# A selective scan on one core: the first stage in an order written by hand, half of a convolution moved into the first scan unit, two row blocks per bank in heads, evictions placed by chunk

## The chip, the cores and the metric

The kernel runs on one core of a Trainium2 chip. Five engines work at once: PE (TensorE) multiplies and transposes, DVE (VectorE), ACT (ScalarE) and POOL (GpSimd) work element by element, and SP (SyncE) issues most of the DMAs. All wait for each other through semaphores. The metric is the time of one execution in microseconds (us); less is better.

## The reference

Layer 0 is a convolutional state space block, layer 1 attention and a mixture of experts. Only layer 0 is touched. Cut to what matters (float32, 4 images of 32 x 32 pixels, 256 channels; Dn = 512, N = 64 states, R = 16):

```python
x = _layernorm(src, ln1_g, ln1_b)
x = x @ w_in + b_in                                   # (4, 32, 32, 512)
x = conv3x3_depthwise(x, conv_w) + conv_b
x = jax.nn.gelu(x).reshape(B, L, Dn)                  # L = 1024
proj = x @ w_x
dt_raw, Bm, Cm = jnp.split(proj, [R, R + N], axis=-1)
dt = jax.nn.softplus(dt_raw @ w_dt + dt_bias)
A = -jnp.exp(A_log)
# over the 1024 pixels:
h = jnp.exp(dt[:, :, None] * A) * h + (dt * x)[:, :, None] * Bm[:, None, :]
y = jnp.einsum('bdn,bn->bd', h, Cm)
# then
y = _layernorm(y + x * D_skip, ln2_g, ln2_b)
out = src + y @ w_out + b_out
```

## The kernel before

**Units and slots.** Work on layer 0 is cut into 8 units: each image has two halves of 512 pixels (`TPB` = 4 row blocks of 128 pixels; `NT` = 8 per image). A unit has 64 states times 4 blocks of 128 channels (`DK` = 4), so 256 slots, and each slot is one scan over 512 pixels on DVE (`scan`, L967). The channels lie on the partitions.

What one slot needs: ACT makes the decay `da` = exp(dt x A) (`decay`, L941) and the scaled input `bx` (`scale`, L921, one per row block of 128 pixels with the pixels on the partitions and 512 channels across); PE turns four 128 x 128 pieces of `bx` into a PSUM bank `ps` (`turn`, L953; there are three such banks); DVE scans; after four slots POOL multiplies the state by C (L978) in one instruction of 128 x 2048; PE adds the result up over the states in four banks `y0` to `y3` (`add_up`, L992). For the first row block of a state, a string `KINDS` says who scales: `A` ACT, `P` POOL (`scale_apart`, L932), `D` PE itself by a diagonal matrix read from DRAM (`turn`, L948; the diagonals are written as entries into `diag_b`, which has to be zero elsewhere).

**The slot loop** (L1126 to L1181) issues the instructions in the order in which they run on each engine; nothing is reordered (`manual_schedule`). Slot k issues `scale` for k + 8, `decay` for k + 4, the scan of k, `add_up` for k − 11 and `turn` for k + 3.

**Work beside the scans.** Between these the loop places pieces of other work for later and earlier units. `beside` makes lists of pieces, each with an engine, an assumed cost and a window of slots (`EVEN`, `ODD`, and `START` for unit 0). `MOST` limits what one slot takes on an engine. Pieces that need a bank all use one, `bg`: "take" claims it, "free" gives it back at the eviction. The pieces are:

- `head(b, g)`: for a half image, rows scaled by the layernorm's 1/sigma (ACT), turned by PE (L339), evicted to `xT` (L344), multiplied by `w_in` (L364), evicted with the bias to `pad` (L375), an image with a border of zeros.
- `conv(v)`: the convolution of unit v as products with diagonal matrices: 9 taps for each of the 4 channel blocks, 36 in all (L417). Three diagonals at a time lie in a tile `dgc` (three buffers). For unit 0 DVE makes them (L401) and they are kept in DRAM as `diags` (L404); later units load them (L406). A tap is 512 wide when the stage runs alone and two of 256 beside scans (`parts`). The result goes to `xg` (L431, L435), then gelu on ACT.
- `dt_bc(w)`: the projections (L470), their turns (L486, L498), dt's products (L541), softplus in several steps (`sum_up` on POOL), the turn of dt x (L595) and its eviction to `dtxT` (L600, L564).
- `after(u)`: layernorm and the product with `w_out` for the unit just ended.

`on_scalar(what)` tells whether an eviction is on ACT or DVE, by its name and the unit's parity (`APART`).

**The first stage** (before the first scan) runs through the same pieces, one list after the other, under a scheduler that works out the order. `late_weights` prepares `w_out`; `head_stats` computes mean and variance of all rows, for the images 1 to 3 from 24 loads of 128 KB.

```python
        head_stats(0, 1)
        run(head(0, 0))
        run(head(0, 1, 0, 1))
        run(conv(0))
        run(head(0, 1, 1, TPB))
        dt_0 = dt_bc(0, None)
        run(*dt_0[:2])
        conv_1 = conv(1)
        ...
        head_stats(1, NB)
        late_weights()
```

`conv(0)` needs half an image and one more row block. `conv(1)` is whole in the first stage, although unit 1 alone needs it. During unit 0 the loop issues `zero_part` on SP, once in each of the first 16 states: a write of 512 KB of zeros into `diag_b`.

Of the kernel before, what the change touches and what calls it, by code (L numbers as in the profile page):

```python
# [33 lines left out]
def conv_ssm_attn_moe_kernel(ctx: ExitStack, tc: tile.TileContext, a: dict, out: bass.AP):  # L34
# [110 lines left out]
    with ExitStack() as l0:  # L145
# [11 lines left out]

        x_0 = pre.tile([P, NT, C], F32, name="x_0", tag="e")
        for g in range(NHALF):
            nc.sync.dma_start(out=x_0[:, blk(g, TPB), :], in_=rows(xf, 0)[:, blk(g, TPB), :])  # L160
        g1 = load_column("L0_conv_ln1_g", CK, w0)
        b1 = load_column("L0_conv_ln1_b", CK, w0)
        w_in = load_rows("L0_conv_w_in", CK, DN, w0)
        b_in = load_column("L0_conv_b_in", DK, w0)
        cw = w0.tile([P, DK, 9], F32, name="cw")
        with nc.allow_non_contiguous_dma(reason="small, once"):
            for m in range(DK):
                nc.scalar.dma_start(
                    out=cw[:, m, :],
                    in_=a["L0_conv_conv_w"][:, :, 0, m * P : (m + 1) * P].rearrange(  # L170
                        "i j p -> p (i j)"
                    ),
                )
        cb = load_column("L0_conv_conv_b", DK, w0)
# [9 lines left out]
        A = load_rows("L0_conv_A_log", DK, NS, w0)  # L184
        nc.scalar.activation(A, A, AF.Exp)
        nc.vector.tensor_scalar(A, A, -1.0, None, ALU.mult)
        dsk = load_column("L0_conv_D_skip", DK, w0)
        g2 = load_column("L0_conv_ln2_g", DK, w0)
        b2 = load_column("L0_conv_ln2_b", DK, w0)
        nc.sync.dma_start(out=w_o, in_=a["L0_conv_w_out"].rearrange("(k p) n -> p k n", p=P))  # L190
        nc.scalar.dma_start(out=b_o, in_=a["L0_conv_b_out"].partition_broadcast(P))
# [16 lines left out]

        pbi = bank()
        for m in range(DK):  # L210
            for ck in range(CK):
                nc.tensor.matmul(
                    pbi[:, m : m + 1], w_in[:, ck, blk(m, P)], b1[:, ck : ck + 1],
                    start=(ck == 0), stop=(ck == CK - 1),
                )
        nc.vector.tensor_tensor(b_in, pbi[:, :DK], b_in, ALU.add)
        centre(w_in, CK, DN, g1)


# [30 lines left out]

        part_of = NS // 8

        def zero_part(i):
            k, n = 1 - i // 8, (i % 8) * part_of
            nc.sync.dma_start(
                out=diag_b[k][n : n + part_of].rearrange("n a b -> a n b"),
                in_=over_middle(zero, part_of),
            )
# [43 lines left out]
        def head_stats(b0, b1):  # L302
            n = (b1 - b0) * NT
            mv = pre.tile([P, n, 2], F32, name="mv_h", tag=f"mv_h{n}")
            for b in range(b0, b1):
                for i in range(NT):
                    t = x_0[:, i, :]
                    if b:
                        t = pre.tile([P, C], F32, name="xs", tag="xr", bufs=2)
                        nc.sync.dma_start(out=t, in_=rows(xf, b)[:, i, :])  # L310
                    variance(mv[:, (b - b0) * NT + i, :], t, C)
            rs = rs_h[:, b0:b1, :].rearrange("p b g -> p (b g)")
            logs(rs, mv[:, :, 1])
            roots(rs, mv[:, :, 1], n)

# [8 lines left out]
        def head(b, g, lo=0, hi=TPB):  # L324
# [11 lines left out]
            def turned(i, ck):  # L336
                if ck == 0:
                    take()
                nc.tensor.transpose(made["bg"][:, blk(ck, P)], made["xn", i][:, blk(ck, P)], ident)  # L339

            def put(i):
                if i == lo:
                    made["xT"] = pre.tile([P, CK, BANK], F32, name="xT")
                (nc.scalar.copy if on_scalar("xT") else nc.vector.tensor_copy)(  # L344
                    made["xT"][:, :, blk(i, P)],
                    made["bg"][:, : CK * P].rearrange("p (k t) -> p k t", k=CK),
                )

            for i in range(lo, hi):
                todo.append(piece(6 if i == lo else 1, "ACT", 0.4, lambda i=i: scaled_rows(i)))  # L350
                todo.append(piece(
                    2, "PE", 0.22, lambda i=i: (turned(i, 0), turned(i, 1)), "take"
                ))
                todo.append(piece(
                    2, "ACT" if on_scalar("xT") else "DVE", 0.42, lambda i=i: put(i), "free"
                ))

            cut = [(lo, hi)] if alone else [(lo, (lo + hi) // 2), ((lo + hi) // 2, hi)]

            def mult(m, ck, i):  # L360
                if ck == 0 and i == 0:
                    take()
                p, q = cut[i]
                nc.tensor.matmul(  # L364
                    made["bg"][:, (p - lo) * P : (q - lo) * P], w_in[:, ck, blk(m, P)],
# [3 lines left out]
            def put_pad(m):  # L369
                pad = pads[m][:, 1 + g * ROWS + lo * RPT : 1 + g * ROWS + hi * RPT, 1 : 1 + WW]  # L370
                bg = made["bg"][:, : (hi - lo) * P].rearrange("p (h w) -> p h w", w=WW)
                if on_scalar("pad"):
# [3 lines left out]

            for m in range(DK):
                for i in range(len(cut)):
                    for ck in range(CK):
                        todo.append(piece(  # L380
                            1, "PE", 1.03 / len(cut), lambda m=m, ck=ck, i=i: mult(m, ck, i),
                            "" if ck or i else "take",
                        ))
                todo.append(piece(
                    3, "ACT" if on_scalar("pad") else "DVE", 0.7, lambda m=m: put_pad(m), "free"
                ))
            return todo

        def conv(v):
# [19 lines left out]
            parts = 1 if alone else 2  # L409
# [14 lines left out]
            def put(m):  # L424
# [3 lines left out]
                if on_scalar("xg"):  # L428
# [13 lines left out]
            for m in range(DK):  # L442
                for k in range(9):
# [10 lines left out]
                    3, "ACT" if on_scalar("xg") else "DVE", 0.69, lambda m=m: put(m), "free"  # L454
# [4 lines left out]
        def dt_bc(w, needs):  # L459
# [15 lines left out]
            def put_pair(j):  # L475
                if j == 0:
                    made["proj", w] = acts.tile([P, TPB, RX], F32, name="proj")
                (nc.scalar.copy if on_scalar("pair") else nc.vector.tensor_copy)(
# [23 lines left out]
            def put_bc():  # L502
# [4 lines left out]
                made["bct", w] = t  # L507
                made["cd", w] = cd
                done.add(("bct", w))

            for j in range(TPB):
# [5 lines left out]
                if j % 2:  # L517
                    todo.append(piece(
                        3, "ACT" if on_scalar("pair") else "DVE", 0.5,
# [59 lines left out]
            def sum_up(m, k):  # L579
                e, dt = made["e"][:, m, :], made["dt", w][:, m, :]  # L580
                eng = nc.vector if alone else nc.gpsimd
                if k == 0:

                    eng.tensor_tensor(e, e, made["s"][:, m % 2, :], ALU.add)
# [14 lines left out]
            def put_dtx(m):  # L599
                (nc.scalar.copy if on_scalar("dtx") else nc.vector.tensor_copy)(  # L600
# [17 lines left out]
            todo = []  # L618
            for m in range(0, DK, 2):
                todo.append(piece(1, "ACT", 1.5, lambda m=m: one_more(m)))  # L620
# [9 lines left out]
            for m in range(DK):  # L630
                todo.append(piece(4 if m == 0 else 1, "PE", 0.44, lambda m=m: turn_dtx(m), "take"))
                todo.append(piece(
                    2, "ACT" if on_scalar("dtx") else "DVE", 0.69,
# [4 lines left out]
        def entries(w):  # L638

            def part(i):  # L640
                with nc.allow_non_contiguous_dma(reason="diagonals"):
                    nc.sync.dma_start(
                        out=diag_b[w % 2].rearrange("n a b -> n (a b)")[
                            blk(i, part_of), :: P + 1
                        ],
                        in_=made["bct", w][blk(i, part_of), :P],
# [20 lines left out]
        def after(u, need):  # L667
# [20 lines left out]
            def put(j):  # L688
                t = pre.tile([P, DK, P], F32, name="yT")
                (nc.scalar.copy if on_scalar("yT") else nc.vector.tensor_copy)(  # L690
# [1544 lines left out]
```

## Time and profile before

| | |
|---|---|
| Time, median of 3 runs | 3336.74 us (3336.47 to 3341.86) |
| Time of the profiled execution | 3336.55 us |
| Its span, first to last instruction | 3334.8 us |
| Mean granted TensorE clock | .989 |
| First stage, to the first scan | 129.06 us |
| Units 0 to 7, from first scan to first scan | 316.67, 321.06, 316.29, 321.46, 316.48, 320.09, 319.62, 308.52 us |
| Layer 1, after the last scan | 665.6 us |

Busy time by stage, from the view of windows (us from the span's start, length, then busy us and number of instructions on each engine, granted clock, share of the DMA engines' time and GB/s):

```profile
core 0: us, PE busy (x) PEld busy (x) DVE busy (x) ACT busy (x) POOL busy (x), PEclk, DMA share, GB/s
0.00:35.40 35.40, 20.90 (x63) 11.75 (x64) 19.54 (x70) 5.14 (x10) 6.16 (x15) 0.90 0.56 131
35.40:66.30 30.90, 30.90 (x75) 13.54 (x74) 16.48 (x63) 0.54 (x2) 1.27 (x5) 1.00 0.43 130
66.30:89.10 22.80, 17.16 (x72) 10.35 (x70) 9.86 (x18) 4.12 (x5) 0.00 (x0) 0.93 0.07 20
89.10:117.40 28.30, 28.24 (x73) 13.12 (x74) 16.04 (x27) 10.47 (x9) 0.00 (x0) 0.94 0.39 115
117.40:129.10 11.70, 11.16 (x40) 6.62 (x38) 4.00 (x12) 11.63 (x16) 2.06 (x3) 1.00 0.00 0
```

These stretches are the head, conv 0, the rest of the head with the projections and dt, conv 1 with softplus beside it, and the last steps to the first scan. "PE" is TensorE's matmuls, "PEld" its loading of weights, which overlaps them. A float32 matmul of 512 columns leaves two records.

### The profile page before, as it was taken

The numbers are of one execution on the slowest core, as the hardware profiler recorded it, in microseconds if no ns is written. First come the engines' busy times: TensorE is split into PE (matmuls) and PEld (weight loads), VectorE is DVE, ScalarE is ACT, GpSimd is POOL, SyncE is SP. The second block draws the span as 40 slices with busy tenths as digits, with TensorE's granted clock in tenths as the row PEclk, the third lists the DMA queues.
The fourth block names the chain that finished last, engine by engine and source line by source line (L and its number), as shares of the span: only waits on it lengthen the run. The fifth ranks groups of instructions, "written<-read, shape, count | busy, mean of one in ns | idle before, by whom it ended". The sixth has DMA issues, their size and how long they took to land.

```text
span 3334.8 us, 62828 instructions
## 1 busy us (share of the span) xinstructions
PE 3158.7 (95%) x23407; PEld 2747.8 (82%) x23407; DVE 2895.5 (87%) x3437; ACT 2716.5 (81%) x4621; POOL 2718.2 (82%) x1216
## 2 busy tenths in 40 slices
PE   7999999999999999999999999989999999899998
PEld 4688988988898888888989888778777766589998
DVE  4799999999999999999999999999999967752222
ACT  1799999999999999999999999999999855322221
POOL 0499998999999989999999999999999943344443
PEclk9999999999999999999999999989999999899999
DMA  4352222222333222233332222322212121477785
GB/s 106 106 120 66 69 67 68 70 70 69 63 77 70 72 69 75 62 67 72 75 72 69 69 66 61 76 52 70 61 59 69 54 66 51 154 198 231 218 252 147
DMA packets 424396, 300.77 MB, mean 90 GB/s; under 512 B 225633, under 2 KB 329953, under 8 KB 424082
## 3 DMA queue, kind: packets, MB, share of 16 engines
q1 hardware_dynamic: 397762, 274.25, 30.1%
q0 software_dynamic: 14016, 18.05, 2.9%
q10 hardware_dynamic: 12304, 4.37, 0.5%
q8 instruction: 187, 3.06, 0.4%
q14 instruction: 127, 1.04, 0.1%
HBM read 262.34 MB, written 34.87 MB: 89 GB/s over the span
## 4 chain that ended last, share of the span: by engine, by line
ACT 42%; PE 37%; DVE 11%; issue 4%; POOL 3%; DMA 2%; SPq 0%; DVEq 0%; POOLq 0%; ACTq 0%
ACT da L941 21%; ACT bx L921 18%; DVE h L967 7%; PE ps L953 7%; PE p L1976 7%; PE y L992 7%; PE pf L1991 3%; PE bg L417 3%; POOL h L978 2%; PE ps L417 2%; PE pqk L1354 1%; PE ps L948 1%; PE ps L364 1%; DMA dgb<-diag_b 1%; PE bg L470 0%
## 5 line engine op out<-in xcount | busy, mean ns | idle before, releaser
L978 POOL TENSOR_TENSOR h<-h,cb_n 128x2048 f32<-128x2048 f32 x511 | 2143.2, 4203 | 117.0 <-DVE h L967 74.7
L941 ACT ACTIVATE da<-dt,l_conv_a_log_sb 128x512 f32<-128x512 f32 x2048 | 1435.5, 712 | 18.6 <-DVE h L967 17.6
L921 ACT ACTIVATE bx<-dtxT,proj 128x512 f32<-128x512 f32 x1748 | 1244.3, 712 | 29.1 <-DVE dtxT L600 16.4
L992 PE MATMUL y<-ident,h 128*128 128x128 f32 x8192 | 1236.1, 274 | 5.8 <-POOL h L978 2.7
L967 DVE TENSOR_TENSOR_SCAN h<-da,last,ps 128x512 f32<-128x512 f32 x1024 | 1217.7, 1258 | 7.2 <-PE ps L953 2.1
L967 DVE TENSOR_TENSOR_SCAN h<-da,ps 128x512 f32<-128x512 f32 x1024 | 1168.9, 1201 | 19.7 <-PE ps L953 7.6
L953 PE MATMUL ps<-ident,bx 128*128 128x128 f32 x6992 | 1117.9, 275 | 41.6 <-DVE h L967 31.1
L992 PEld LDWEIGHTS y<-ident,h 128*128 128x128 f32 x8192 | 978.9, 141 | 96.0 <-issue 20.0
L953 PEld LDWEIGHTS ps<-ident,bx 128*128 128x128 f32 x6992 | 820.0, 142 | 100.0 <-DVE h L967 82.0
L1983 DVE TENSOR_TENSOR hT<-s,p 128x256 f32<-128x256 f32 x146 | 61.5, 421 | 276.7 <-ACT s L1982 248.7
L2001 POOL DMA_INDIRECT out_dram<-yb,src x73 | 116.0, 1589 | 204.0 <-DVE yb L1998 71.9
L953 PE MATMUL ps<-ident,bxp 128*128 128x128 f32 x800 | 236.4, 295 | 44.9 <-DVE h L967 32.4
L1982 ACT ACTIVATE s<-p 128x256 f32<-128x256 f32 x146 | 56.1, 384 | 260.8 <-PE p L1976 239.7
L417 PE MATMUL bg<-pad,dgc 128*128 128x256 f32 x864 | 258.1, 380 | 0.6 <-DMA dgc<-diags 0.6
L953 PEld LDWEIGHTS ps<-ident,bxp 128*128 128x128 f32 x800 | 112.1, 140 | 125.9 <-DVE h L967 74.1
L932 POOL TENSOR_SCALAR bxp<-dtxT,proj 128x512 f32<-128x512 f32 x200 | 141.2, 706 | 59.3 <-DVE dtxT L600 59.3
L948 PE MATMUL ps<-dgb,dtxT 128*128 128x128 f32 x800 | 171.4, 296 | 19.1 <-DMA dgb<-diag_b 9.2
L1976 PE MATMUL p<-xT,w 128*128 128x128 f32 x1408 | 173.5, 277 | 2.2 <-ACT xT L1956 2.2
L1976 PEld LDWEIGHTS p<-xT,w 128*128 128x128 f32 x1408 | 169.0, 193 | 5.1 <-ACT xT L1956 3.0
L948 PEld LDWEIGHTS ps<-dgb,dtxT 128*128 128x128 f32 x800 | 120.5, 190 | 46.7 <-DVE h L967 34.3
L417 PEld LDWEIGHTS bg<-pad,dgc 128*128 128x128 f32 x864 | 130.5, 191 | 0.8 <-DMA dgc<-diags 0.8
L1976 PE MATMUL p<-xT,m 128*128 128x128 f32 x928 | 113.2, 275 | 0.0
(343 smaller groups left out, 2675.4 us busy)
## 6 DMA issues: line engine op xcount, KB each, us to landing
cb_n<-cd SPq DMA_DIRECT2D x512, 256.0 KB
m<-in_L_ffn_w_dram SPq DMA_DIRECT2D x87, 512.0 KB
w<-in_L_ffn_w_dram SPq DMA_DIRECT2D x60, 512.0 KB
dgc<-diags SPq DMA_DIRECT2D x84, 192.0 KB
diag_b<-zero SPq DMA_DIRECT2D x16, 512.0 KB
dgb<-diag_b SPq DMA_DIRECT2D x100, 64.0 KB
last<-h SPq DMA_DIRECT2D x256, 2.0 KB
xd<-xe SPq DMA_DIRECT2D x8, 512.0 KB
```

Of the source, the lines that this page charges most:

```text
L417: nc.tensor.matmul(made["bg"].rearrange("p (h w) -> p h w", w=WW)[:, blk(c, deep), :], made["dgc", m * 3 + i][:, j, :], pads[m][:, at : at ...
L921: nc.scalar.activation(t, made["dtxT", u][:, j, :], AF.Copy, scale=made["proj", u][:, j, R + n : R + n + 1])
L932: nc.gpsimd.tensor_scalar(t, made["dtxT", u][:, 0, :], made["proj", u][:, 0, R + n : R + n + 1], 1.0, ALU.mult, ALU.mult,)
L941: nc.scalar.activation(t, made["dt", u][:, m, :], AF.Exp, scale=A[:, m, n : n + 1])
L948: nc.tensor.matmul(t[:, blk(j, P)], made["dtxT", steps[s][0]][:, j, blk(m, P)], made["dgb", s], start=True, stop=True,)
L953: nc.tensor.transpose(t[:, blk(j, P)], made["bx", s, j][:, blk(m, P)], ident)
L967: nc.vector.tensor_tensor_scan(h[:, m, 1:], made.pop(("da", s, m)), made.pop(("dbx", s, m)), 0.0 if seg == 0 else last[b][:, n, m : m + 1] ...
L978: nc.gpsimd.tensor_tensor(h[:, :, :BANK], h[:, :, 1:], over_middle(made["c", s], DK), ALU.mult)
L992: nc.tensor.matmul(made["y", u][j][:, blk(m, P)], made["h", s][:, m, blk(j, P)], ident, is_transpose=True, start=n == 0 and m == 0, stop=n ...
L1976: nc.tensor.matmul(p12[:, j, s, :], w_of(w, key)[:, ck, blk(h + j, P)], on_b["xT", key][:, ck, :], start=(ck == 0), stop=(ck == CK - 1),)
L1991: nc.tensor.matmul(on_b["pf", key], on_b["hT", key][:, hk, :], w_of("w3", key)[:, hk, :], start=(hk == 0), stop=(hk == HK - 1),)
L2001: s = nc.gpsimd.indirect_dma_start(of[:, :], bass.IndirectOffsetOnAxis(src[:, c : c + 1], 0), yb, None, bounds_check=NB * L - 1, oob_is_er ...
```

## The change

**The first stage** is written out by hand, under `manual_schedule`. The first half of the image is loaded, then `w_in`, then the second half; `cw` is loaded on SP's queue instead of ACT's; ACT's table is loaded first; small loads come later. `w_in` is scaled into `w_s` and centred from there. The rows are scaled in place, and two blocks share a bank when turned (`turn_x0`). Each channel block is evicted by ACT and DVE in turn (`put_rows`). In conv 0, `triple` issues three taps; beside them stand the statistics of the other images' rows, now loaded in 12 DMAs of 256 KB into the scan's ring (`other_rows`), the 16 zero writes (two after each of the first six triples, then one), the turns of the late rows and `late_weights`. Gelu reads PSUM directly, block by block, and the projections are accumulated block by block (`project_0`). Softplus is split over ACT, DVE and POOL. Of conv 1, two channel blocks (18 taps) fill PE's gaps (`filler`).

**Unit 0.** The other 18 taps of conv 1 are a new list `rest` in slots 11 to 20, with taps 512 wide. The zero writes are gone from the slot loop. Two of the first `bx` are made by DVE.

**Heads** turn two row blocks into one bank and evict both at once: two evictions of 128 x 512 instead of four of 128 x 256.

**Placing.** `on_scalar` takes the chunk as well (`pad1`, `xT3`), and `APART` has a third row for unit 0. `KINDS` has a row for unit 0 (37 states on POOL, 29 before), and two other rows are edited. Most windows of `EVEN`, `ODD` and `START` move; POOL's limit in `MOST` is 1.1. In unit 1's softplus ACT's step is done one channel block at a time.

```diff
+        nc.scalar.preload_act_table_set("natural_log_exp_and_others")
         x_0 = pre.tile([P, NT, C], F32, name="x_0", tag="e")
...
-            for i in range(lo, hi):
-                todo.append(piece(6 if i == lo else 1, "ACT", 0.4, lambda i=i: scaled_rows(i)))
+            for i in range(lo, hi, 2):
+                n = min(2, hi - i)
...
+                todo.append(piece(2, "PE", 0.22 * n, lambda i=i, n=n: turned(i, n), "take"))
                 todo.append(piece(
-                    2, "PE", 0.22, lambda i=i: (turned(i, 0), turned(i, 1)), "take"
+                    2, "ACT" if on_scalar("xT", i) else "DVE", 0.1 + 0.3 * n,
+                    lambda i=i, n=n: put(i, n), "free",
                 ))
...
-            parts = 1 if alone else 2
+            parts = 1 if alone or v in (1,) else 2
...
-            return not alone and what in APART[made["u"] % 2]
+            return not alone and f"{what}{part}" in APART[made["u"] % 2 if made["u"] else 2]
...
-            return 2 if u + 1 == len(units) else u % 2
+            return 3 if u == 0 else 2 if u + 1 == len(units) else u % 2
...
                 if u == 0:
+                    rest = conv(1)
+                    cut = [i for i, p in enumerate(rest) if p[4] == "free"][PRE_CONV - 1] + 1
                     lists.append([
-                        (head(b, 0), at["head"]), (head(b, 1), at["head1"]), (conv(v), at["conv"]),
+                        (rest[cut if PRE_CONV else 0 :], at["rest"]), (head(b, 0), at["head"]),
+                        (head(b, 1), at["head1"]), (conv(v), at["conv"]),
                     ])
...
-            'ADADAAPAAAPAAAPAAAPADAPADAAAAPPPDAPADAPADAPAADADDPPPDPPPDPPPDAPA',
+            'ADADAAPAAAPAAAPAAAPADAPADPPPDPPPDPPPPAADAPAADADDPPPAPPPDPPPDAPA',
+            'DPPPPPPAPPPPPPPPPPPPPPPPAPPPPPPAAAAPAAPAAAPAAAAAAAAAAPAPAPAPAPAP',
...
         START = {
-            'skip': (13, 54),
-            'head': (11, 36),
-            'head1': (44, 75),
-            'conv': (43, 228),
+            'skip': (54, 126),
+            'rest': (11, 20),
+            'head': (16, 88),
+            'head1': (90, 102),
+            'conv': (120, 248),
...
+        def triple(m, i, ps):
+            q = 3 * m + i
+            if q + 2 < 3 * DK:
+                taps_0[q + 2]()
+            for j in range(3):
+                nc.tensor.matmul(
+                    ps.rearrange("p (h w) -> p h w", w=WW), made["dgc", q][:, j, :],
+                    pads[m][:, i : i + ROWS, j : j + WW],
+                    start=(i + j == 0), stop=(i + j == 4),
+                )
+
+        for b in range(1, NB):
+            other_rows(b)
+        zeros = iter(range(16))
+        late = None
+        for m in range(DK):
+            ps = spare(m)
+            for i in range(3):
+                triple(m, i, ps)
+                at = NT + 2 * (3 * m + i)
+                for t in range(at, min(at + 2, NB * NT)):
+                    variance(mv_h[:, t, :], row_of(t), C)
+                for _ in range(2 if m < 2 else 1):
+                    for t in (next(zeros, None),):
+                        if t is not None:
+                            zero_part(t)
...
+            nc.scalar.activation(xg[:, m, :], ps, AF.Gelu_apprx_tanh, bias=cb[:, m : m + 1])
+            if m == 1:
+                pp = spare(0), ps_w.tile([P, BANK], F32, name="bg", tag="bg", bufs=1)
+                project_0(0)
+            elif m == 2:
+                project_0(1)
+                for k in range(DK):
+                    t = bank()
+                    project_in(k, t[:, : (TPB - 1) * P], xT_2, 1, TPB)
+                    put_rows(k, TPB + 1, NT, t[:, : (TPB - 1) * P], k % 2)
+            elif m == 3:
+                project_0(2)
...
+        filler(11)
+        cd = made["cd", 0] = dram0.tile([NS, BANK], F32, name="cd")
+        nc.sync.dma_start(out=cd, in_=last_of[NS:, :])
+        for s in range(4):
+            fetch(s)
+        turn_dtx0(1)
+        filler(2)
...
-                if k % DK == 2 and k // DK < 16:
-                    zero_part(k // DK)
```

## The prediction

> **What bounds the kernel now.** I read first the page's engine totals and costliest groups. The groups give three rows that the sum uses again and again.
>
> ```profile
> PE 3158.7 (95%) x23407; PEld 2747.8 (82%) x23407; DVE 2895.5 (87%) x3437; ACT 2716.5 (81%) x4621; POOL 2718.2 (82%) x1216
> ...
> L941 ACT ACTIVATE da<-dt,l_conv_a_log_sb 128x512 f32<-128x512 f32 x2048 | 1435.5, 712 | 18.6 <-DVE h L967 17.6
> L921 ACT ACTIVATE bx<-dtxT,proj 128x512 f32<-128x512 f32 x1748 | 1244.3, 712 | 29.1 <-DVE dtxT L600 16.4
> ...
> L967 DVE TENSOR_TENSOR_SCAN h<-da,ps 128x512 f32<-128x512 f32 x1024 | 1168.9, 1201 | 19.7 <-PE ps L953 7.6
> ```
>
> PE's 95% doesn't say what a stage is worth, so I cut the span at the first scan of each unit (129.06, 445.72, 766.78 and so on) with the view of windows. Units 0 to 2:
>
> ```profile
> core 0: us, PE busy (x) PEld busy (x) DVE busy (x) ACT busy (x) POOL busy (x), PEclk, DMA share, GB/s
> 129.06:445.72 316.66, 298.19 (x2333) 268.15 (x2334) 310.34 (x289) 314.87 (x503) 299.33 (x106) 0.99 0.37 89
> 445.72:766.78 321.06, 310.62 (x2455) 280.45 (x2453) 318.41 (x287) 314.48 (x509) 304.36 (x111) 1.00 0.25 70
> 766.78:1083.07 316.29, 305.89 (x2433) 278.05 (x2432) 310.11 (x295) 310.37 (x501) 309.12 (x119) 1.00 0.31 70
> ```
>
> ACT is idle 1.8 us in unit 0, DVE 2.6 in unit 1, every engine at least 5.9 in unit 2. The scan phase is full on four engines: it gains only what its fullest engine loses. The first stage, before 129.06, is another matter. The timeline of PE:
>
> ```profile
> 22.45 9.77 PE L364 MATMUL ps<-xT,l_conv_w_in_sb 128*128 128x512 f32 x16 [1.01 <-DVE xT L344]
> ...
> 71.82 7.12 PE L364 MATMUL ps<-xT,l_conv_w_in_sb 128*128 128x384 f32 x16 [0.52 <-DVE xT L344]
> 78.78 4.08 PE L470 MATMUL ps<-l_conv_w_x_sb,xg 128*128 128x144 f32 x32
> ...
> 89.06 25.14 PE L417 MATMUL ps<-pad,dgc 128*128 128x512 f32 x54 [0.67 <-DVE e L553]
> 114.04 2.26 PE L595 MATMUL ps<-ident,e 128*128 128x128 f32 x16
> 116.24 7.99 PE L417 MATMUL ps<-pad,dgc 128*128 128x512 f32 x18
> 124.07 1.89 PE L235 MATMUL ps<-l_conv_w_out_sb,b2w 128*128 128x256 f32 x8
> 125.79 1.89 PE L203 MATMUL ps<-l_conv_w_out_sb,every 128*128 128x256 f32 x8
> ```
>
> Here one engine works while the others wait. PE is the chain, and conv 1, 36 taps in the rows of 25.14 and 7.99 us, is not needed by any scan of unit 0.
>
> **First stage, to the start of conv 0 (35.36 before).** Afterwards weight centring (L203, 3.71 us at 14.06) and bias products (L212, 3.58 us at 10.33) run back to back as soon as w_in is scaled: w_in lands at 10.3, a scaling takes some .4, so PE is busy 10.7 to 18.0. The table load that held rs to 16.1 (12.79 to 14.07, behind ACT's loads) now precedes, so rows are scaled by then. Turns and one eviction 1.2, then eight 512-wide products at .863 (the 72 tap records of conv 0 last 31.07, two a tap) and eight 128-wide at .216, 8.6 together: conv 0 starts at 27.8. In the trace the granted clock is .5 from 20.97 to 27.8, and the 512-wide products took 9.77 for 6.9. If the half clock covers one 3.4 us stretch of them the start is 31; if part of 10.7 to 18.0 is at full clock, 26.
>
> **Conv 0.** Taps 31.1, turns of late rows .7, half the project products 2.0 (L470, 4.08 in all), the remaining heads, eight 384-wide at three quarters of .863, 5.2, w_o 3.8 (the two 1.89 rows), steps behind DVE 1.0: 43.8. Added is a wait for dgc. A dgc buffer (three) is free when its write to diags has landed, and SP's queue now holds in front of those writes twelve loads of 256 KB of other rows (packets of 56 ns, 16 at a time: .92 each, 11.0 in all) and twelve of the sixteen 512 KB zero writes. Those the trace shows in unit 0 alone:
>
> ```profile
> core 0: us, PE busy (x) PEld busy (x) DVE busy (x) ACT busy (x) POOL busy (x), PEclk, DMA share, GB/s
> 142.70:200.00 57.30, 56.14 (x484) 53.98 (x484) 57.06 (x55) 57.30 (x97) 57.22 (x22) 1.00 0.68 180
> 245.00:302.30 57.30, 51.90 (x390) 46.07 (x391) 54.68 (x53) 56.15 (x86) 49.89 (x16) 0.97 0.25 59
> ```
>
> Twelve of them raise the DMA share by .43 over 57.3 us, 2.05 us of all queues each; their packet records (1024 of 27 ns over 16) give 1.73. With z for that price, dgc 8 needs the rows, six zero writes and four diags writes (.52 each): 27.5 + 11 + 6z + 2.1 + 2.5 for landing and making = 43.1 + 6z (a dgc takes DVE .7, three instructions of 279 ns; landing 1.8 by estimate, from the 1.45 that DVE waited for a row load in conv 0). Its turn on PE is at 27.8 + 8 × 2.59 + .7 + 1.0 = 50.2. The wait is 6z − 7.1: 3.3 or 5.2, and I take 4.2. Bounds 0 (they overlap better) and 10 (z of 2.85). The last dgc needs twelve: 12z − 23.4, nothing at these prices. Conv 0 ends at 27.8 + 43.8 + 4.2 = 75.8.
>
> In unit 0 of the trace no wait names a zero write; the longest that a load ends there is .8 (a dgc). Read so, the wait would be 0 and the sum 4.2 lower. [...]
>
> **To the first scan.** Project 2.0, eviction .5, turns .5, dtr .7, dt products 3.8 (L541), eighteen taps of conv 1 15.5, dtx turns 2.0, bank waits .6, first turn .5: 26.1. Softplus (ACT about 10, DVE 12 us at .59 to .69 each) runs beside the taps. Bounds 24, without waits, and 30, if softplus isn't covered. First scan at 101.9 for 129.06: **−27.2**.
>
> **Unit 0.** The other eighteen taps are now in slots 13 to 34, one a slot, 512 wide. A slot costs PE .44 (turn) + .44 (add-up) + .863 = 1.74, the scan 1.132 (its back-to-back interval). Summed in the new order of instructions slot by slot, PE falls 8.2 behind DVE there, and 6.5 in the later conv; before, 5.4 in the one conv. Three banks of PSUM let PE be some 1.6 late. So the stalls are 6.6 + 4.9 = 11.5 for 3.8: +7.7. ACT stands still meanwhile, and it was full, so nothing is made up. Gone are table loads at slots 106 to 127 (DVE idle 2.5 there, one pair fewer, −2.0) and DVE work: eight xT evictions of .319 become two of .593 with two on ACT, two pads of .64 fewer, one xg and one projection more, −1.65. One gelu more +.4. Sum +4.5; 0 if the burst is absorbed by ACT's lead of eight bx, +9 if ACT's added work (311.8 to 314.4 by count) doesn't fit beside it.
>
> The zero writes leave unit 0; at nothing, since no wait there names them.
>
> **Other units.** Units 1, 3, 5: two xT evictions of 512 for eight of 256 and two xg fewer, −1.4 of DVE, which is the bound; but PE's one lag of 3.4 becomes two of 3.2, +1.4 beyond the lead of 1.6 each. ACT gains 1.1. I take −.5 each, −1.5 (bounds −4.2 and +1). Units 2 and 4: −1.4 on DVE, PE's lag 7.6 to 9.4, +1.8; POOL +.7: +.5 each, +1.0 (−1 to +3). Unit 6 +.3, unit 7 and the later layers 0.
>
> Sum −27.2 + 4.5 − 1.5 + 1.0 + .3 = −22.9. The profiled execution lasted 3336.55, .2 below the median of the runs, 3336.74: **3313.6**.
>
> **Rivals.** *PE pays twice* (0.15): the first stage is less covered, first scan near 107, or unit 0 gives back 9 and the even units 3. For it: ACT and PE are both above 94% in unit 0. Against: the stage's serial PE work is plainly less. 3313.6 + 5 + 4.5 = 3323, and 3328 with the other units at their bounds. *The burst is absorbed* (0.15): stalls at slots 13 to 34 vanish and DVE's −1.4 counts whole in odd units: −4.5 − 2.7 − 2.0 (wait in conv 0 half as long) = 3304, down to 3300. For it, unit 0's chain is ACT (da 43%, bx 39%), not PE; against, ACT too stops when no bank is read. *Zero writes gate conv 0* (0.08; slower side): each occupies the queue for the 4.8 us at which they follow each other in unit 0. Then the last dgc waits 12 × 4.8 − 23.4 = 34, 30 more than forecast: 3343.6. It decides against the change from z = 4.2. Against it, twelve at a time raised the share by .43, not to 1; it gets 0.04 beyond slower and 0.04 between. *The change doesn't do what it says*: its instructions stand as described in the new order, so no chance.
>
> **How the numbers follow.** Forecast 0.62. Its own range is 3306 to 3322, the bounds above added as squares (low 1.8, 4.2, 2, 4.5, 2.7, 2: 7.5; high 3.2, 5.8, 4, 4.5, 2.5, 2: 9.5). The range, 3301 to 3326, takes most of both faster rivals. Two runs can't be told apart under .2%, 6.7 us: faster below 3330.1: .62 + .15 + .15 = 0.92; same 0.04; slower, over 3343.4, 0.04.
>
> **What would show it.** Conv 0's first tap at about 28 and its last dgc late by 4; first scan at 102; POOL, ACT and DVE busy inside it. PE with no idle at the taps of the first unit and DVE waiting for PE ps some 7 us at slots 13 to 34; unit 0 at 321; odd units within 1 us. Wrong would be: a first scan past 110 with idle PE at dgc; unit 0 under 317 (burst absorbed) or over 326; odd units changed by over 2.

## The result, and the profile after

The changed kernel took 3324.30 us (median of 6 runs, 3321.07 to 3327.40), the kernel before 3337.66 (6 runs, 3336.47 to 3341.86): a ratio of 0.996, 95% interval 0.995 to 0.997. That is 13.4 us less; 23 were forecast. The time is inside the stated range of 3301 to 3326, but above the forecast's own 3306 to 3322, at the place of the first rival (3323 to 3328).

By span (3334.8 to 3323.0, 11.8 us less) the difference divides at the first scan of each unit:

| Stage | before | after | change | forecast |
|---|---|---|---|---|
| First stage, to the first scan | 129.06 | 114.42 | −14.6 | −27.2 |
| Unit 0 | 316.67 | 323.38 | +6.7 | +4.5 |
| Units 1, 3, 5 | 962.6 | 960.7 | −1.9 | −1.5 |
| Units 2, 4 | 632.8 | 633.6 | +.9 | +1.0 |
| Unit 6 | 319.62 | 316.76 | −2.9 | +.3 |
| Unit 7 and layer 1 | 974.0 | 974.1 | +.1 | 0 |

The view of windows for units 0 and 1 (columns as before):

```profile
114.42:437.81 323.39, 308.51 (x2374) 273.31 (x2372) 308.68 (x283) 315.15 (x506) 304.97 (x114) 1.00 0.30 66
437.81:759.55 321.74, 311.70 (x2454) 282.22 (x2452) 318.21 (x283) 317.22 (x514) 303.93 (x111) 0.99 0.25 70
```

In unit 0 ACT has as much to do as before (315.15 to 314.87) but is idle 8.2 us instead of 1.8, and PE's work has grown by 10.3. The shortfall is in the first stage. Its windows: to the last in-projection product, conv 0 with the gap before its first tap, the projections and dt, and two stretches with taps of conv 1:

```profile
0.00:29.90 29.90, 20.82 (x62) 13.00 (x62) 8.48 (x25) 6.28 (x13) 5.78 (x15) 1.00 0.38 86
29.90:83.40 53.50, 43.60 (x128) 22.01 (x128) 28.02 (x111) 6.94 (x13) 1.18 (x5) 1.00 0.93 270
83.40:92.80 9.40, 8.96 (x33) 4.43 (x31) 3.90 (x6) 5.90 (x10) 2.23 (x2) 0.78 0.08 24
92.80:105.00 12.20, 11.94 (x27) 5.30 (x26) 11.71 (x14) 5.50 (x13) 8.57 (x9) 0.75 0.16 44
105.00:114.40 9.40, 9.32 (x32) 4.85 (x33) 2.38 (x4) 6.28 (x12) 2.48 (x3) 1.00 0.52 174
```

Two things stand out. The second window lasts 53.5 with PE idle 9.9 of them, and the DMA engines are nearly full (share .93, 270 GB/s). And from 83.4 to 105 PE is hardly ever idle (.44 and .26 us), yet its granted clock is .78 and .75: by the clock's records it was halved from 88.72 to 98.96. The 1.00 of the first window is no measurement as a whole: the clock's records begin at 23.87, and the view counts time without a record as 1.00. That PE ran slowly there too is read from its timeline, in which four records of 512 columns take 3.75 us early and 1.88 later; the last three rows are dt's products and the first taps of conv 1, under the halved clock:

```profile
18.30 3.75 PE L1153 MATMUL y<-xT,l_conv_w_in_sb 128*128 128x512 f32 x4 [0.79 <-DVE l_conv_w_in_sb L1184]
...
27.61 1.88 PE L1153 MATMUL y<-xT,l_conv_w_in_sb 128*128 128x512 f32 x4
...
87.19 4.01 PE L1319 MATMUL ps<-dtr,w_dt 17*128 17x512 f32 x6 [0.33 <-DVE dtr L1305]
91.01 1.91 PE L1319 MATMUL y<-dtr,w_dt 17*128 17x512 f32 x2
92.84 10.16 PE L400 MATMUL bg<-pad,dgc 128*128 128x512 f32 x16
```

What PE waited for in conv 0 (view of waits: engine, what waited, for what, us in total, times, longest):

```profile
DVE dgc L384 <- DMA diags<-dgc: 17.5, 7, 7.5
...
PE y L1230 <- DVE dgc L384: 6.7, 4, 3.4
...
PE ps L225 <- DVE b2w L222: 2.3, 1, 2.3
```

PE waits 6.7 us for the diagonals, DVE makes them late because the buffer's write to `diags` hasn't landed, and `b2w` (an operand that `late_weights` makes) is late because it stands on DVE behind the last of them. The timeline of PE shows where:

```profile
32.35 10.54 PE L1230 MATMUL y<-pad,dgc 128*128 128x512 f32 x24 [2.41 <-DVE dgc L384]
...
49.29 2.84 PE L1230 MATMUL y<-pad,dgc 128*128 128x512 f32 x6 [3.39 <-DVE dgc L384]
...
56.12 2.84 PE L1230 MATMUL y<-pad,dgc 128*128 128x512 f32 x6 [0.21 <-DVE dgc L384]
59.64 2.84 PE L1230 MATMUL y<-pad,dgc 128*128 128x512 f32 x6 [0.68 <-DVE dgc L384]
```

The 2.41 at the start is no matter of queues: DVE does statistics of rows 5 to 7 (30.34 to 31.95) before the first `dgc` (31.95 to 33.2). The 3.39 is the sixth triple's. Its `dgc` takes the buffer of the third, whose write stands on SP's queue behind the twelve row loads (timeline of SP):

```profile
33.60 9.78 SPq L1118 DMA_DIRECT2D h<-in_x_dram  x12
43.48 0.41 SPq L387 DMA_DIRECT2D diags<-dgc  x1
```

### The profile page after: what moved, and what is told of

The parts are those of the page before. It is cut to its first block, busy times and chain, and to the rows that moved or that the text cites. A ratio compares the mean times of both kernels' runs of the same rounds, so it can differ in the third digit from the quotient of the medians.

```text
span 3323.0 us, 62819 instructions
## 1 busy us (share of the span) xinstructions
PE 3155.1 (95%) x23403; PEld 2748.6 (83%) x23403; DVE 2873.4 (86%) x3387; ACT 2719.7 (82%) x4643; POOL 2736.8 (82%) x1242
## 4 chain that ended last, share of the span: by engine, by line
ACT 46%; PE 37%; DVE 10%; issue 3%; DMA 2%; POOL 0%; SPq 0%; DVEq 0%; POOLq 0%; ACTq 0%
ACT da L917 23%; ACT bx L899 19%; PE ps L929 8%; PE y L968 7%; PE p L2249 7%; DVE h L943 6%; PE bg L400 4%; PE pf L2264 3%; PE pqk L1627 2%; DMA diags<-dgc 1%; PE ps L924 1%; PE y L976 1%; DMA out_dram<-yb,src 1%; PE bg L524 0%; PE px L2227 0%
## 5 line engine op out<-in xcount | busy, mean ns | idle before, releaser
L400 PE MATMUL bg<-pad,dgc 128*128 128x256 f32 (+1 forms) x936 | 296.1, 400 | 2.2 <-ACT xg L412 1.8
L929 PE MATMUL ps<-ident,bxp 128*128 128x128 f32 x864 | 253.5, 293 | 39.7 <-DVE h L943 29.0
L929 PEld LDWEIGHTS ps<-ident,bxp 128*128 128x128 f32 x864 | 120.9, 140 | 118.6 <-DVE h L943 73.7
L908 POOL TENSOR_SCALAR bxp<-dtxT,proj 128x512 f32<-128x512 f32 x216 | 152.9, 708 | 9.0 <-DVE dtxT L1357 7.8
L400 PEld LDWEIGHTS bg<-pad,dgc 128*128 128x128 f32 x936 | 143.4, 192 | 12.3 <-issue 9.4
```

Source lines behind the costliest of these rows:

```text
L400: nc.tensor.matmul(made["bg"].rearrange("p (h w) -> p h w", w=WW)[:, blk(c, deep), :], made["dgc", m * 3 + i][:, j, :], pads[m][:, at : at ...
L908: nc.gpsimd.tensor_scalar(t, made["dtxT", u][:, 0, :], made["proj", u][:, 0, R + n : R + n + 1], 1.0, ALU.mult, ALU.mult,)
L929: nc.tensor.transpose(t[:, blk(j, P)], made["bx", s, j][:, blk(m, P)], ident)
```

## The experiments

Each is an edit on the changed kernel, but for e11, which is one on the kernel before. The table holds all runs: the time (median), and from the one profiled execution of each the first tap of conv 0, the end of its taps (where PE's next product starts), the first scan, the stretches of half clock between first tap and first scan, and units 0 and 6.

| Run | time (runs) | first tap | taps end | first scan | half clock | unit 0 | unit 6 |
|---|---|---|---|---|---|---|---|
| before | 3337.66 (6) | 35.36 | 66.3 | 129.06 | 3.4 + 3.4 | 316.67 | 319.62 |
| after | 3324.30 (6) | 32.35 | 83.4 | 114.42 | 10.2 | 323.38 | 316.76 |
| e1 zeros back | 3320.44 (4) | 30.88 | 81.0 | 110.40 | 6.8 + 6.8 | 323.42 | 315.90 |
| e2 dgc early | 3311.61 (4) | 29.50 | 76.0 | 107.07 | 10.2 | 323.39 | 316.69 |
| e3 taps among dt | 3320.73 (4) | 30.41 | 84.5 | 113.53 | 6.8 | 323.41 | 317.64 |
| e4 conv 1 first | 3343.93 (10) | 31.02 | 82.3 | 127.82 | 3.4 + 3.4 + 3.4 | 326.30 | 316.37 |
| e5 short taps | 3313.10 (1) | 30.90 | 82.3 | 110.31 | 6.8 + 3.4 | 316.56 | 316.65 |
| e6 row mean on ACT | 3316.33 (4) | 32.82 | 84.7 | 112.67 | 6.8 + 3.4 | 323.43 | 311.54 |
| e7 one block | 3320.35 (1) | 29.41 | 81.4 | 110.80 | 3.4 + 3.4 + 6.8 | 323.47 | 317.99 |
| e8 warm | 3322.95 (4) | 29.46 | 82.6 | 111.95 | 3.4 + 6.8 + 6.8 | 323.42 | 318.08 |
| e9 all | 3306.52 (5) | 25.63 | 70.0 | 99.00 | 3.4 | 323.45 | 312.65 |
| e10 all, cold | 3310.31 (5) | 29.74 | 74.1 | 105.48 | 10.2 | 323.39 | 311.97 |
| e11 before, row mean on ACT | 3333.43 (10) | 33.99 | 64.9 | 129.82 | 6.8 + 6.8 | 316.67 | 313.63 |

One caution for all that follows: e5, e6 and e7 leave the first stage as it was, and their first scan still stands at 110.31, 112.67 and 110.80 for 114.42 after. So a single profile can't tell a first scan 4 us earlier from none. The same holds of their first taps (29.41 to 32.82). e5 and e7 ran once, so their times carry no verdict. Units 2, 4 and 7 agree within .5 from run to run, as does unit 0 but for e4 and e5; unit 1 is about 320.3 or 321.8, unit 6 315.9 to 318.1 where its instructions are the same.

**e1: the zero writes back in unit 0.**

```diff
-                for _ in range(2 if m < 2 else 1):
-                    for t in (next(zeros, None),):
-                        if t is not None:
-                            zero_part(t)
...
+                if k % DK == 2 and k // DK < 16:
+                    zero_part(k // DK)
```

> The sixteen zero writes are back in unit 0, one a state, as before the change; all else as changed. Theory (the queue gates conv 0): PE's waits for dgc in conv 0 (3.4, .2 and .7 us) fall to under 1, DVE's waits for the diags writes with them, conv 0 ends 4 to 5 us earlier (79 instead of 83.4), the first scan stands near 110 instead of 114.4, and unit 0 stays at 323 within 1: the whole is 4 us faster than the changed kernel, about 3320. Rival (the twelve loads of other rows gate it, not the zero writes): the waits stay above 3 and the first scan above 113. Second rival (the zero writes cost unit 0 as much): unit 0 goes to 326 or more and the time stays.

The long wait did not go: PE waited 2.4 at the start and 4.26 in the sixth triple, in the timeline of PE:

```profile
48.70 5.15 PE L1230 MATMUL y<-pad,dgc 128*128 128x512 f32 x6 [4.26 <-DVE dgc L384]
```

The small ones behind it did (.21, .68, and 2.35 for `b2w`), and the DMA share in conv 0 fell from .92 to .39. Unit 0 stayed at 323.4, so the zero writes cost it nothing. The median fell by 3.9 us, as the theory said, but neither that nor the first scan shows it: the ratio to before is 0.9949 (0.9932 to 0.9965), which overlaps that of the changed kernel, and unchanged first stages also end at 110.3. It is the waits that show the theory half right: the zero writes held up the later diagonals, the other rows' loads the first.

**e2: the first diagonals early.**

```diff
         variance(mv_h[:, TPB, :], x_0[:, TPB, :], C)
+        taps_0 = [p[3] for p in conv(0) if p[1] == "SP"]
+        for i in range(2):
+            taps_0[i]()
         root_h(0, TPB + 1)
...
-        conv_0 = conv(0)
-        taps_0 = [p[3] for p in conv_0 if p[1] == "SP"]
-        for i in range(2):
-            taps_0[i]()
```

> The first two dgc are made as soon as cw is there, before the statistics of rows 5 to 7 instead of after them; the other rows' loads, behind them on SP's queue, then start near 12 us instead of 33.6. Theory: the 2.4 us between the last in-projection product and the first tap vanish (conv 0 starts at 30.0 instead of 32.35), and with 3 MB out of the way of the diags writes the wait of 3.4 in the sixth triple falls under 1; the first scan stands near 108 to 110. Rival (PE's start is set by something else, or the loads now delay w_o, w_x and the second half image): conv 0 starts after 31.5 or the first scan stays within 1 of 114.4.

The waits went as expected, and the first scan came one us earlier than that. The row loads are issued from 13.6 instead of 33.6, and PE finds its diagonals, although all sixteen zero writes are still in conv 0. The timeline of PE from the first tap:

```profile
29.50 5.32 PE L1229 MATMUL y<-pad,dgc 128*128 128x512 f32 x12
35.66 5.42 PE L1229 MATMUL y<-pad,dgc 128*128 128x512 f32 x12 [0.84 <-DVE dgc L384]
```

First tap to end of taps takes 46.5 instead of 51.0. The wait of the sixth triple, .7 to 4.3 in the eight profiles in which the rows are loaded late, is gone here and in e9 and e10. The ratio is 0.9919 (0.9902 to 0.9935), below that of the changed kernel without overlap: 12.7 us between the medians, more than the 7.4 by which the first scan moved in the two profiles. The profiled executions themselves differ by 6.3 (3325.27 and 3318.97): e2's was its slowest run, and what its other three did 7 to 10 us faster stands in no profile.

**e3: taps among dt's products.**

```diff
+        filler(2)
         for m in range(DK):
...
             raws.append(t)
+            if m < 3:
+                filler(1)
...
-        filler(11)
+        filler(6)
```

> Three taps of conv 1 stand between the products of dt (one before the first, one after each of the first two) instead of after them. Theory (the granted clock of .5 from 88.7 to 99.0 comes of a stretch in which PE does turns and products of 17 rows alone, and costs 5 us): the clock stays at 1.0 or is halved for one stretch of 3.4 us at most; the first scan stands near 110 to 111, 4 us earlier. Rival (softplus is the chain, the clock hides behind it): dt's products end 2 us later and the first scan stands at 114 to 116.

In this profile the clock stayed at full speed through dt's products, as the theory said, but the gain was 2.1 (taps' end to first scan 29.0 for 31.1), not 4: PE then waited 2.15 us for softplus on DVE, as the rival said. Another half clock, after the `b2w` wait (73.2 to 80.0), lies in conv 0, which lasted 54.1 for 51.0. That the taps held the clock isn't shown by one profile: in e10, with the same taps in the same place, it was halved for 10.2 us. In time e3 (0.9948, 0.9931 to 0.9964) can't be told from the changed kernel.

**e4: all of conv 1 in the first stage** (`PRE_CONV = 4` for 2).

> All 36 taps of conv 1 are in the first stage; only its gelu is left in unit 0's list. Theory (the moved half saved its 15.5 us of PE in the first stage and gave some 6.5 back as scans that wait for PE in slots 18 to 35): first scan at 130 (+15.5), unit 0 at 317 (-6.5), the time 9 us above the changed kernel, about 3333. Rival (unit 0's extra time comes of the other edits to its order): unit 0 stays above 321, and the time is 14 or more above.

The first scan came 13.4 us later than after. But unit 0 grew, to 326.3. Its stalls at slots 18 to 35 fell from 6.4 to 2.7 us, less than expected; 10.6 us of new ones came at slots 135 to 144, for which the view of waits names a load:

```profile
PE bg L400 <- DMA dgc<-diags: 8.0, 1, 8.0
```

No other run of the changed kernel shows that wait. With `rest` nearly empty the lists behind it move up, and SP's queue stood at this point with `cb_n` and `last` before the load; that this delayed it is argued from the order alone. The time is 19.6 us above the changed kernel's and above the one before (1.002, 1.001 to 1.0029), and unit 0 stays above 321. These are the signs that the rival named, but here they come with a wait that the move itself brought. So this run prices the first stage, and not unit 0.

**e5: short taps in unit 0.**

```diff
+                r = 4 if v == 1 and m >= 2 and k else deep
...
-                    pads[m][:, at : at + deep, j : j + WW],
+                    pads[m][:, at : at + r, j : j + WW],
```

> Left out: of the eighteen taps of conv 1 that stand in unit 0, sixteen multiply a quarter of their pixels (128 columns instead of 512). PE then needs some 1.1 us in each of those slots instead of 1.74, no more than the scan; dgc loads, evictions and all positions stay. Theory (the scans of slots 18 to 35 wait for PE, 6.4 us in the changed kernel): DVE's idle time there falls under 1 and unit 0 to 317 from 323.4; the stalls at slots 44 to 61 and 152 to 248 stay. Rival (those scans wait for ACT, the gelu table or dgc loads, PE's work only lies beside): the idle time stays above 4 and unit 0 above 321.

Unit 0 fell to 316.56, and DVE's idle time at slots 18 to 35 from 6.4 us to none. The same view of waits, to the first quarter of unit 0, after and in e5:

```profile
DVE h L943 <- PE ps L929: 8.5, 12, 3.4
```

```profile
DVE h L944 <- PE ps L930: 4.0, 2, 3.4
```

The 3.4 in both is the wait before the first scan. Without it the scans wait 5.1 us in eleven places in the one and .6 in one place in the other. PE's burst is the price of the move, and about as large as all that unit 0 grew by (6.8 and 6.7).

**e6 and e11: row means on ACT**, e6 on the changed kernel, e11 on the kernel before.

```diff
-                nc.vector.tensor_scalar(m, m, -1.0 / C, None, ALU.mult)
+                nc.scalar.activation(m, m, AF.Copy, scale=-1.0 / C)
```

> The three scalings of 128 x 2 row means in unit 6 (6.0 us for two, 3.4 for the third on DVE in the changed kernel; 13.1 and .2 before the change) are done by ACT. Theory (a DVE instruction of this form stands until POOL's 4.2 us instruction beside it ends, so its length is a matter of where it falls, and unit 6's -2.9 is such a matter): ACT takes .2 to .4 for each, unit 6 goes from 316.8 to 310 to 312, where POOL's 310 us bound it, and the time falls by 5 to 7. Rival (the long time hides a wait for the reduction before it): ACT's instruction starts as late as DVE's ended, and unit 6 stays at 316 to 317.

> The kernel before the change with its three row means in unit 6 on ACT, nothing else. Theory (the long instructions on DVE have nothing to do with the change): unit 6 from 319.6 to 311 to 313, all other units and the first scan (129.1) as before, the time 7 to 8 us below the kernel before, about 3330. Rival (the gain in unit 6 needs the change's own order there): unit 6 above 316.

ACT takes .19 for each:

```profile
L772 ACT ACTIVATE w_mean<-w_mean x2: 186/187/188, 2174.2 to 2201.0; 128x2 f32<-128x2 f32 x2
```

Unit 6 fell from 316.76 to 311.54 in e6 (3316.33 us, a ratio to before of 0.9935, 0.9918 to 0.9952, which just meets the changed kernel's) and from 319.62 to 313.63 in e11, whose time was 3333.43 (10 runs), a ratio of 0.9984 (0.9974 to 0.9993): 5.2 us by median where 7 to 8 were expected. In the kernel before, the timelines of DVE and POOL show what the long instruction stood for:

```profile
2182.24 5.73 DVE L775 TENSOR_SCALAR w_mean<-w_mean 128x2 f32<-128x2 f32 x1
...
2212.87 7.38 DVE L775 TENSOR_SCALAR w_mean<-w_mean 128x2 f32<-128x2 f32 x1
...
2243.74 0.20 DVE L775 TENSOR_SCALAR b_mean<-b_mean 128x2 f32<-128x2 f32 x1
```

```profile
2182.50 4.21 POOL L978 TENSOR_TENSOR h<-h,cb_n 128x2048 f32<-128x2048 f32 x1
2186.62 1.31 POOL L588 TENSOR_TENSOR dt<-dt,e 128x512 f32<-128x512 f32 x1
...
2239.73 4.18 POOL L978 TENSOR_TENSOR h<-h,cb_n 128x2048 f32<-128x2048 f32 x1
```

The first ends at 2187.97, POOL's run of instructions at 2187.93. The second ends at 2220.25 with POOL's run at 2220.22. The third took .20: it began .17 before POOL's 4.18 us instruction ended, and ended .03 after it. So their length is a matter of where they fall: 13.3 us together before, 9.4 after. But unit 6's −2.9 isn't explained by that alone. With the means on ACT in both kernels it is still 1.0 to 2.1 us shorter after the change (313.63 in e11; 311.54, 312.65 and 311.97 in e6, e9 and e10), and it differs by 2.2 between profiles with the same instructions.

**e7: one row block per bank in odd units** (`range(lo, hi)` with `n = 1` there).

> Heads in units 1, 3 and 5 turn one row block per bank again (four evictions of 128 x 256 instead of two of 128 x 512); even units and the rest stay as changed. Theory (the eviction's count hardly matters: 4 x .32 against 2 x .59 us): units 1, 3 and 5 stay within .5 of 321.7, 320.2 and 318.7, so what they gained comes of the evictions that went from DVE to ACT. Rival (fewer claims on the one background bank are what the change gained there): odd units longer by 1 to 2 each.

Units 1, 3 and 5 took 320.01, 320.00 and 318.67, no longer than after (321.74, 320.25, 318.67). Pairing the blocks shows no gain there. Even units and unit 0 were not tried.

**e8: PE kept busy at the start.**

```diff
+        warm = bank()
+        for i in range(36):
+            nc.tensor.matmul(warm[:, :P], every, every, start=True, stop=True)
```

> 36 products of a 128 x 128 tile of ones that nothing reads stand on PE before the weight centring, where PE is idle from 1.7 to 8.3 us. Theory (the half clock costs the first stage 3 to 5 us up to the last in-projection product, 29.9 in the changed kernel): the products L1172 and L1176 take 4 us instead of 7.2, the first 512-wide ones 1.9 instead of 3.75, the in-projection ends at 25 to 27, the first scan stands near 111, and the time falls by 3 to 4. Rival (the start is set by the loads of w_in, cw and the rows, and by DVE's order): the first tap stays after 31.5 and the first scan within 1 of 114.4.

The clock was full from 6.36; weight centring took 1.88 for 3.78, the bias products 1.84 for 3.41. The 36 products ran to 12.2 and kept the centring waiting, so the in-projection ended at 27.0 for 29.9 and the first tap came at 29.46. In time it is inconclusive: 0.9955 (0.9939 to 0.9972) against 0.996.

**e9 and e10: the edits together**, e9 with 22 products of ones (6.8 us), e10 without.

> All five edits together on the changed kernel: zero writes back in unit 0, the first two dgc early, three taps of conv 1 among dt's products, row means on ACT, and 22 products of ones ahead of the weight centring. Theory (each took away its own wait): first tap at 27, conv 0 without a wait for dgc over 1 us, first scan near 102 to 104 (forecast for the change itself: 101.9), unit 6 at 311.5, units 0 to 5 as changed; time 3303 to 3308. Rival (the first stage is one chain in which the waits only move on to softplus or to a halved clock): first scan 106 or later, time above 3309.

> The same without the products of ones. Theory (the half clock at the start costs PE some 3 us up to the first tap): first tap at 29.5, first scan 2 to 3 us after that of the run with them, time 2 to 3 us more. Rival (a colder start only shifts where the clock falls later): both within 1 us.

e9 took 3306.52 (5 runs, 3306.03 to 3311.50), a ratio of 0.9903 (0.9887 to 0.9918): 17.8 us less than the changed kernel, 31 less than the one before. The view of waits has 5.3 us for PE in its whole first stage, the first 1.7 among them; the five longest:

```profile
PE ps L1162 <- DVE every L198: 1.7, 1, 1.7
PE y L1153 <- DVE l_conv_w_in_sb L1190: 0.9, 1, 0.9
PE ps L205 <- DVE l_conv_w_out_sb L202: 0.9, 1, 0.9
PE y L1232 <- DVE dgc L384: 0.8, 1, 0.8
PE y L1355 <- DVE e L1348: 0.5, 1, 0.5
```

The first scan stands at 99.0, earlier than the 101.9 forecast for the change itself. e10 took 3310.31, a ratio of 0.9913 (0.9898 to 0.9928): 3.8 us more by median, a little more than expected, with intervals that overlap. Its profile differs by 6.5 at the first scan, of which 4.1 are at the first tap and the rest a longer half clock among dt's products.

## Why the prediction was right, and where it was off

**Direction and range.** The first stage was a chain of PE's work, half of conv 1 left it, and unit 0 paid for it with scans that wait for PE. That is how it went. The number was right with some luck: the time lies above the forecast's own range (its bounds add up to 3323 at the top, not 3322) and inside the stated one only because that was widened for the rivals. By the prediction's own signs its first stage was wrong: the first scan came past 110, with PE idle for `dgc`. Of the five terms outside the first stage three were within 1 us (the odd units' sum, the even units', unit 7), though unit 1 moves by 1.4 from run to run.

**Unit 0.** Stalls of 11.5 us for 3.8 were counted, +7.7, less 2.0 for idle time at table loads; DVE was idle 14.7 for 6.3, +8.4. The burst was sized well: slots 18 to 35 have 6.4 us for .2, 6.6 were forecast, and e5 shows PE's taps as the cause. The idle time at slots 106 to 127 went from 2.6 to nothing, as forecast. DVE's work fell by 1.66 for 1.65. The step that failed is the stalls beside the later conv, counted at 1.1 us more than before: slots 152 to 248 have 6.7 us for 2.9, most of it at slots 162 to 182 (4.2 for .3), and slots 44 to 61 have 1.2 for none. The view of waits at slots 162 to 182 after the change:

```profile
DVE h L943 <- ACT da L917: 2.8, 4, 1.0
DVE h L943 <- PE ps L929: 1.2, 2, 1.0
```

Two thirds of it is a wait for ACT, which the forecast looked for on PE. In these slots ACT does steps of softplus (`s`) and an eviction of `xg`, and no table load; no run tests which of them is the cause. Hence 6.7 for 4.5. (The scan's back-to-back interval in the trace is 1.11 us, since four in a row last 4.53 and one 1.20, and not 1.132; that changes the burst by .4 in eighteen slots.)

**The first stage: 12.5 us too good**, in three steps. (By the earlier first scans of e5, e6 and e7, with the same first stage, it would be 8.4 to 10.8.)

- *Start of conv 0: 27.8 forecast, 32.35 measured.* The products of the in-projection began at 18.3 where 19.2 was counted, and took 11.6 for 8.6, the first 5.6 of that before the clock's first record, at half speed (four records in 3.75 for 1.88); that was inside the bound of 31. The other 2.4 are in no step: that DVE would do three rows' statistics ahead of the first `dgc` could be read in the order of instructions. e2 takes it away.
- *Conv 0: 48.0 with a wait of 4.2 forecast, 51.0 measured.* The waits for `dgc` after the first came to 4.3: the size was right by luck, the cause only half. The forecast looked for it at dgc 8, behind six zero writes; it came at dgc 5, behind the twelve row loads, which SP issues from 33.6 to 43.4. e1 (no zero writes, wait still there) and e2 (rows earlier, zero writes still there, wait gone) tell the two apart. That the zero writes would hold up PE here, when no wait in unit 0 had named one, was the author's estimate, and no run shows its price of 4.2: without them (e1) 3.2 us of waits went, at two later `dgc` and at `b2w`, and the sixth triple's grew by .9. Of the 3.0 too much 2.2 are `b2w` and the centring of w_o, which wait 3.2 where 1.0 was allowed for steps behind DVE; the rest is PE's own work, 43.5 us for 42.8.
- *To the first scan: 26.1 forecast, 31.1 measured.* The sum took every PE duration at full clock. The clock was halved for 10.2 us: eight taps took 10.16 instead of 6.9, dt's products 5.7 instead of 3.8. That is the 5 us.

The last is the most instructive. The forecast bounded a half clock at the start alone, where PE first stands idle (10.33 us in the kernel before). From 83.4 PE was busy 8.96 of 9.40 us, and from 88.72 to 98.96 all of 10.24, at half clock all the same; in the kernel before it was halved too after dt's products (89.2 to 92.7), in a row that the forecast had at hand. In this stretch PE turns 128 x 128 blocks and multiplies matrices of 17 rows. e3 put three full taps among them and the clock held, and in e9 it was halved for 3.4 us only; in e10, with the same taps, for 10.2 again. Without them it was halved for 3.4 us only in e4, e5 and e6 too. So it isn't shown that the mixture helps, and what halves the clock here stays open.

Every whole stretch in the clock's records of before and after lasts 3.41 us or a multiple of it, and the half clocks in the table, of thirteen profiles, last 3.4, 6.8 or 10.2. With the same first stage (after, e5, e6, e7) the first half clock behind the first tap begins at 88.72, 46.58, 48.47 and 29.77, so the order of instructions alone doesn't tell where it falls.

**Unit 6** had +.3 in the forecast and moved by −2.9: the 13.3 us of three 128 x 2 instructions in the profile before were seen as unchanged work. Little of that was work: the third took .20, on ACT each takes .19 (e6), and all six of these instructions, before and after, end .03 to .04 us after the end of one of POOL's. What held them until then no run shows, and three of them stood through several of POOL's instructions.

**The rivals.** "PE pays twice" had the time and the half of its story that is about the first stage; units 2 and 4 paid only .9 and unit 0 6.7 of the 9 supposed. "The burst is absorbed" fell with e5. "Zero writes gate conv 0" was real in kind, far from its price: in e1 3.2 us of PE's waits went and .9 came back at the sixth triple.

**What stays open:** why e2's time fell by 5 us more than its first scan; what makes unit 1 take 320.3 or 321.8; what DVE waits for at slots 162 to 182 of unit 0; which part of unit 6's −2.9 is the change's; whether taps among dt's products hold the clock; and e4's 8 us load.

## What to carry to other kernels

A chain of PE's work is not a sum of full-speed durations: here eight taps behind dt's products took 10.16 us for 6.9, with PE busy all the while. So look in the profile for the granted clock after stretches of transposes and thin products, busy or not, and carry those rows into the sum. A buffer that is refilled only when its write to DRAM has landed can tie PE to what stands on the queue in front of that write (3.39 us at the sixth triple behind twelve row loads; no wait there in e2, where the loads are issued from 13.6 instead of 33.6), so bulk loads belong on the queue before the loop begins or after it. And a tiny instruction with a long time can be a wait (7.38 us on DVE for 128 x 2 values, .19 on ACT): see what the neighbouring engine was doing when it ended.

## What the runs showed of the hardware that was not expected

- The granted clock fell to .5 with PE busy 95% of 9.4 us (turns, 144-column and 17-row products), and in all eight profiles of the changed first stage in which dt's products follow one another it was halved for 3.4 to 10.2 us during or after them.
- A DVE multiplication of 128 x 2 values stood 5.73 and 7.38 us while POOL ran instructions back to back, through the end of one and the whole of the next two or three, and .20 when it began .17 us before the end of one; on ACT it takes .19.
- Sixteen writes of 512 KB in conv 0 raised the DMA share from .39 in e1 to .92 after (54 us, 115 to 268 GB/s), and by its waits PE lost only 2 to 3 us by them.
